# Batches of two key tiles in a sparse attention, and a routing table in buffers of its own

## The chip, the cores and the metric

The kernel runs on one core of a Trainium2 chip. The metric is the device time of one execution in microseconds (us). Before the change the median of three runs is 2298.0 us (2296.09 to 2302.13). The profiled execution, on which all readings of the trace rest, spans 2318.8 us.

The core has five engines that run side by side and meet through semaphores: TensorE (PE, with its weight loads PEld listed apart), VectorE (DVE), ScalarE (ACT), GpSimd (POOL) and SyncE (SP), which here only starts transfers. SBUF is the working memory with 128 partitions; PSUM takes what TensorE writes, in banks of 128 x 512 floats, of which the attention's pools use eight; HBM is the memory outside.

## The reference

One layer: attention of 4096 nodes over the neighbours that an adjacency matrix names, and then a mixture of experts, each with a layer norm ahead and a residual.

```python
# attention; x is (4096, 512), 8 heads of 64, adj is 0/1 and sparse
adj = jnp.maximum(adjacency_matrix, eye)
q, k, v = (jnp.einsum('nd,hdk->hnk', norm(x), W) for W in (Wqs, Wks, Wvs))
scores = jnp.einsum('hqk,hmk->hqm', q, k) * kd ** (-0.5)
scores = scores + IDENTITY_BIAS * eye - MASK_VAL * (1.0 - adj)
att = jax.nn.softmax(scores, axis=-1)
x = x + jnp.einsum('hqm,hmk,hko->qo', att, v, Wo)
# mixture: 8 experts, two for each token, hidden size 512
logits = xf @ Wg + bg                                   # xf = norm(x)
topk_scores, topk_idx = jax.lax.top_k(logits, 2)
topk_w = jax.nn.softmax(topk_scores, axis=-1)
h = gelu(einsum('nd,edh->neh', xf, W1) + b1)            # exact gelu
y = einsum('neh,ehf->nef', h, W2) + b2
x = x + sum over the two chosen experts of topk_w * y
```

All numbers are 32-bit floats.

## The kernel before

It has three stages.

**Stage one** projects q, k and v, stores them in HBM, and makes for each of the 32 tiles of 128 queries a list of the nodes that are a neighbour of any of them. The list is cut into tiles of 128 keys. A tile of keys whose nodes are wanted by the first 64 queries alone, or by the last 64 alone, is a *half* step; the others are *full* steps. How many tiles each query tile has is fixed in the program:

```python
LISTED = [28, 20, 18, 16, 15, 14, 13, 13, ... 8, 8]       # tiles of keys, 363 in all
FIRST_ALONE = [10, 6, 5, 5, 4, ... 2, 2]    # tiles c < this: first half of the queries
SECOND_FROM = [25, 14, 12, 10, 10, ... 5, 5]    # tiles c >= this: second half
```

That gives 229 half steps and 134 full ones. Each query tile also begins with its own 128 nodes (c = -1), a full step: 395 steps.

**Stage two** is the attention. Keys and values are gathered row by row by GpSimd from HBM (`kv`), the adjacency as a mask with them; PE turns the keys (`pk`), ACT copies them to SBUF (`kT`), PE makes the scores (`s`), ACT their exponentials (`e`), DVE masks them and adds them up for the denominators (`acc`), and PE multiplies them with the values into `po`.

```python
AHEAD = 9                                     # kv and mask tiles: 10 buffers
items = [(i, c) for i in range(NT) for c in range(-1, listed[i])]
# PSUM banks: ps_s 3, ps_o 1, ps_k 2 (one tile of two banks), ps_e 2

def turn(n):                                  # keys of one step
    pk = ps_k.tile([P, 2, TB], F32, tag="k", name=f"pk_{n}")
    for p in range(NP):                       # 8 transposes
        for r in range(2):
            half = slice(r * KD, (r + 1) * KD)
            nc.tensor.transpose(
                pk[:, r, ts(p, KD)], kv[n][half, ts(p, P)], ident[half, half])
    nc.scalar.copy(kT[n]..., pk[:, :, : NP * KD]...)

def scores(n):
    if full:                                  # two banks, 64 rows of the array each
        s = [ps_s.tile([P, NP, P], ...) for r in range(2)]
        for p in range(NP):
            for r in range(2):
                rows = slice(r * KD, (r + 1) * KD)
                nc.tensor.matmul(s[r][:, p, :], k[rows, p, :], q_in[i][rows, p, r, :], ...)
        for r in range(2):
            nc.scalar.activation(e...[:, r], s[r], AF.Exp)
    else:                                     # one bank, the whole array, q with zeros
        s = ps_s.tile([P, NP, 2, QH], F32, tag="s", name=f"s_{i}_{c}")
        for p in range(NP):
            nc.tensor.matmul(s[:, p], k[:, p, :], q_in[i][:, p, :, q], ...)
        nc.scalar.activation(e, s.rearrange("p a r q -> p (a r) q"), AF.Exp)

def masked(n):
    nc.vector.tensor_mul(e, e, m.unsqueeze(1).to_broadcast(e.shape))

def values(n):
    if c < 0:
        po[i] = ps_o.tile([P, NP, P], F32, tag="o", name=f"po_{i}")
    for h in range(H):                        # 8 products, 64 columns of the array each
        p, r = divmod(h, 2)
        nc.tensor.matmul(po[i][r * KD : (r + 1) * KD, p, q], v[:, ts(h, KD)], e[:, h, :], ...)
    if c >= 0:
        nc.vector.tensor_add(acc[i][:, :, q], acc[i][:, :, q], e)

for n, (i, c) in enumerate(items):            # the order of the instructions
    begin()
    if n + AHEAD < len(items):
        fetch(n + AHEAD)                      # gathers kv, gathers or loads the mask
    ...
    if c < 0 and i:                           # a new query tile: po of the last one goes out
        osb[i - 1] = single.tile([P, NP, P], F32, tag="o", name=f"o_{i - 1}")
        nc.scalar.copy(osb[i - 1], po.pop(i - 1))
    turn(n + 3); scores(n + 2); values(n)
    later(n)                                  # one piece of the work after a query tile
    masked(n + 2)
```

The pieces after a query tile (`later`) are the sums over `acc`, their reciprocals, `rb`, the product `py` with Wo, the residual, and the routing of the tile's tokens: each token is written to `xs_d` in HBM, once into the region of either expert that it chose (regions of N + 128 rows).

**Between stages two and three** a table says which expert and which 128 rows each of 69 blocks takes. An expert's last block is seldom full, so the rows after its last token are overwritten with blank rows, which point to spare rows of the output. Then a check decides whether the attention has to be done again in a plain way (it isn't with these inputs).

```python
with tc.tile_pool(name="end", bufs=1) as pool, tc.tile_pool(
    name="ps_end", bufs=1, space=PSUM) as psum:
    finish_routing(pool, psum, blank)         # about 20 instructions of DVE, and:
    #   nc.sync.dma_start(out=xs_d[E * R : E * R + P, :], in_=blank)
    #   for e in range(E):
    #       last = nc.values_load(table[:, 2 * NB + e : ...], engines=(SP,), ...)
    #       s = nc.sync.dma_start(out=xs_d[bass.ds(last, P), :], in_=blank)
again = nc.values_load(redo, ...)
with tc.If(again > 0):
    ...
```

**Stage three** takes block by block: load 128 rows (`r`), turn them, multiply by W1, gelu, turn, multiply by W2, weigh, and add to the output with a scatter of GpSimd.

Of the kernel before, what the change touches and what calls it, by code (L numbers as in the profile page):

```python
# [20 lines left out]
P = 128  # L21
# [22 lines left out]
def kernel(  # L44
# [106 lines left out]
    nc.gpsimd.iota(start_e, pattern=[[R, E]], base=0, channel_multiplier=0,  # L151
# [3 lines left out]
    for e in range(1, E):  # L155
# [9 lines left out]
    nth = const.tile([P, NB], F32, name="nth")  # L165
    nc.gpsimd.iota(nth, pattern=[[1, NB]], base=0, channel_multiplier=0,
                   allow_small_or_imprecise_dtypes=True)
# [4 lines left out]
    table = const.tile([1, 2 * NB + E], I32, name="table")  # L172
# [39 lines left out]
    AHEAD = 9  # L212
    items = [(i, c) for i in range(NT) for c in range(-1, listed[i])]
# [21 lines left out]
    def gather_mask(m, i, c):  # L235
        if half_of(i, c) is None:
            gather(m, adjT_rows, mask_of, i, c)
        else:
            gather(m[:, :QH], adjT_halves, mask_of, i, c)
# [4 lines left out]
    def mask_part(m, i, c):  # L244
        return m if half_of(i, c) is None else m[:, :QH]

    def fetch(n):

        i, c = items[n]
        kv[n] = kvp.tile([P, KV], F32, tag="kv", name=f"kv_{i}_{c}")  # L250
        mask[n] = kvp.tile([P, P], F32, tag="mask", name=f"mask_{i}_{c}")
        if c < 0:
            nc.sync.dma_start(out=kv[n], in_=kv_d[ts(i, P), :])
            nc.sync.dma_start(out=mask[n], in_=adjT[i, ts(i, P), :])
            return
        gather(kv[n], kv_d, key_of, i, c)
        if (i, c) in packed:
            nc.sync.dma_start(out=mask_part(mask[n], i, c), in_=packed_at(i, c))
        else:
            gather_mask(mask[n], i, c)  # L260

        if waiting and n % 3 == 0:
            waiting.pop(0)[1]()
# [9 lines left out]
    with tc.tile_pool(name="wqkv", bufs=1) as wp, tc.tile_pool(name="p1", bufs=3) as work, tc.tile_pool(  # L273
# [347 lines left out]
        nc.sync.dma_start(out=out[N : N + P, :], in_=blank[:, :D])  # L621

# [4 lines left out]
        def pack():  # L627
            i, c = ready.pop(0)
            m = work.tile([P, P], F32, tag="mask", bufs=5, name=f"pm_{i}_{c}")
            gather_mask(m, i, c)  # L630
            packed[i, c] = len(packed)
            nc.sync.dma_start(out=packed_at(i, c), in_=mask_part(m, i, c))
# [4 lines left out]
        for u in range(8 * NTB + 1):  # L637
# [38 lines left out]
            if u - 3 in load_at:  # L676
                neighbours(load_at[u - 3])
                if load_at[u - 3] == NT - 1:

                    ap_cm.__exit__(None, None, None)  # L680
                    kv_cm = tc.tile_pool(name="kv", bufs=AHEAD + 1, side="right")
# [9 lines left out]
                    fetch(0)  # L691
            if u == 8 * NTB - 4:
                for n in range(1, AHEAD):
                    fetch(n)
# [115 lines left out]
    def finish_routing(pool, psum, blank):  # L810
# [26 lines left out]
        )  # L837
        expert = pool.tile([P, NB], F32, name="expert")
# [4 lines left out]
        nc.vector.tensor_scalar_mul(first, first, float(P))  # L843
# [5 lines left out]
        nc.vector.tensor_add(many, many, start_e)  # L849
        nc.vector.tensor_copy(table[:, :NB], expert[:1])  # L850
        nc.vector.tensor_copy(table[:, NB : 2 * NB], first[:1])
        nc.vector.tensor_copy(table[:, 2 * NB :], many[:1])
        nc.vector.tensor_add(first, first, number.to_broadcast([P, NB]))

        nc.sync.dma_start(out=xs_d[E * R : E * R + P, :], in_=blank)
        for e in range(E):
            last = nc.values_load(
                table[:, 2 * NB + e : 2 * NB + e + 1], engines=(SP,), min_val=e * R,
                max_val=e * R + N, skip_runtime_bounds_check_because=why,
            )  # L860
            s = nc.sync.dma_start(out=xs_d[bass.ds(last, P), :], in_=blank)
            for t in scatters:
                tc.declare_no_dep(s.ins, t.ins, reason="other rows")
            scatters.append(s)
# [602 lines left out]
```

## Time and profile before

| what | where | us |
|---|---|---|
| median of the runs | times | 2298.0 |
| span of the profiled execution | page | 2318.8 |
| stage one, to the first turned key of stage two | trace, PE | 0 to 449 |
| stage two, to the end of the last value product | trace, PE | 449 to 1715 |
| end of the routing, table, check, first rows | trace, PE | 1715 to 1764 |
| stage three | trace, PE | 1764 to 2311 |

The page gives each engine's busy time over the span, the span in 40 slices, the chain that ended last, and groups of equal instructions with count, busy time, mean duration of one and the engine's idle time just before them. A timeline row of PE joins neighbouring matmuls of one kind: its start, the time from the first start to the last end, and how many. One 32-bit matmul of the program shows as two records. The chain that ended last holds only the final scatter here, so the stages are read from windows and timelines.

### The profile page before, as it was taken

How to read it: one execution, taken by the hardware profiler on the slowest of the kernel's cores; microseconds unless marked ns; L12 is line 12 of the kernel's file. 1: busy time of each engine (PE TensorE's matmuls, PEld its weight loads, DVE VectorE, ACT ScalarE, POOL GpSimd, SP SyncE). 2: the span in 40 equal slices, each digit the busy share in tenths (PEclk: the TensorE clock that was granted, in tenths of full speed). 3: DMA queues.
4: the chain of work that ended last, by engine and by line, in shares of the span. 5: the costliest groups of instructions: out<-in, count | busy, mean ns of one | idle time of the engine just before them, and what ended most of it. 6: DMA issues, size and time to landing. Idle time of an engine off the chain costs nothing. (4 is left out here: it accounts for less than half of the span.)

```text
span 2318.8 us, 48467 instructions
## 1 busy us (share of the span) xinstructions
PE 2104.1 (91%) x18748; PEld 1395.4 (60%) x18748; DVE 1262.0 (54%) x2289; ACT 928.4 (40%) x1703; POOL 1020.0 (44%) x1078
## 2 busy tenths in 40 slices
PE   7988987899999889999999899999975999999997
PEld 3434443487777767777777777777752444444443
DVE  4786666176666656655656666565662323232322
ACT  2544443354545445445445454444531222222221
POOL 1043445666666555555565655556630212211212
PEclk9999999899999899999999999999987999999999
DMA  7778787666777777777787777766766565655554
GB/s 289 314 269 262 258 274 247 204 207 201 228 237 232 209 226 228 219 208 220 220 232 225 239 207 217 234 200 202 203 212 173 134 140 129 135 132 133 136 138 91
DMA packets 213232, 479.04 MB, mean 207 GB/s; under 512 B 49106, under 2 KB 81106, under 8 KB 208900
## 3 DMA queue, kind: packets, MB, share of 16 engines
q0 software_dynamic: 78944, 241.65, 37.2%
q1 hardware_dynamic: 132900, 232.10, 32.6%
q8 instruction: 153, 2.51, 0.4%
q10 hardware_dynamic: 1152, 2.10, 0.3%
q14 instruction: 83, 0.68, 0.1%
HBM read 398.85 MB, written 76.90 MB: 205 GB/s over the span
## 5 line engine op out<-in xcount | busy, mean ns | idle before, releaser
L230 POOL DMA_INDIRECT kv<-kv_d,key_of x363 | 402.8, 1110 | 414.6 <-PE po L993 228.7
L981 DVE TENSOR_TENSOR e<-e,mask 128x512 f32<-128x512 f32 (+1 forms) x363 | 322.2, 888 | 321.8 <-ACT e L973 150.1
L926 ACT COPY kT<-pk 128x512 f32<-128x512 f32 x395 | 232.3, 588 | 375.5 <-PE pk L923 209.7
L993 PE MATMUL po<-e,kv 128*64 128x64 f32 (+1 forms) x5808 | 327.2, 251 | 24.0 <-issue 23.1
L999 DVE TENSOR_TENSOR acc<-acc,e 128x512 f32<-128x512 f32 (+1 forms) x363 | 320.9, 884 | 3.3 <-PE pk L923 2.5
L230 POOL DMA_INDIRECT mask<-in_adjT_dram,mask_of x234 | 280.0, 1197 | 72.9 <-issue 66.7
L1394 POOL DMA_INDIRECT out_dram<-y,r x69 | 107.5, 1557 | 463.8 <-issue 191.3
L993 PEld LDWEIGHTS po<-e,kv 128*64 128x64 f32 x5808 | 254.9, 140 | 76.5 <-issue 33.1
L970 PE MATMUL s<-q,kT 128*128 128x128 f32 x1832 | 283.9, 300 | 2.2 <-issue 1.8
L1358 PE MATMUL ph<-w,xT 128*128 x552 | 251.6, 599 | 0.7 <-ACT xT L209 0.7
L970 PEld LDWEIGHTS s<-q,kT 128*128 128x128 f32 x1832 | 237.4, 202 | 20.0 <-issue 3.5
L1387 PE MATMUL py<-w,hT 128*128 x552 | 248.4, 593 | 0.9 <-DVE hT L1372 0.9
L923 PE MATMUL pk<-ident,kv 64*128 64x64 f32 x2904 | 177.8, 240 | 43.4 <-issue 21.5
L923 PEld LDWEIGHTS pk<-ident,kv 64*128 64x128 f32 x2904 | 124.6, 142 | 114.4 <-issue 77.1
L230 POOL DMA_INDIRECT pm<-in_adjT_dram,mask_of x129 | 125.0, 969 | 155.2 <-DMA packed_h<-pm 73.9
L361 DVE TENSOR_REDUCE flags<-adjT 128x64 f32<-128x4096 f32 x32 | 141.1, 4411 | 67.4 <-DMA adjT<-in_adjT_dram 67.3
L963 ACT ACTIVATE e<-s 128x512 f32<-128x512 f32 x268 | 146.9, 597 | 72.9 <-PE po L993 28.6
L973 ACT ACTIVATE e<-s 128x512 f32<-128x512 f32 x229 | 137.9, 602 | 90.7 <-PE s L970 55.8
L958 PE MATMUL s<-q,kT 64*128 64x128 f32 x2144 | 164.0, 284 | 3.8 <-issue 2.3
L1392 DVE TENSOR_TENSOR y<-py,bb 128x512 f32<-128x512 f32 x69 | 47.7, 692 | 219.2 <-PE py L1387 209.7
L1358 PEld LDWEIGHTS ph<-w,xT 128*128 128x128 f32 x552 | 100.5, 192 | 101.3 <-issue 100.2
L1387 PEld LDWEIGHTS py<-w,hT 128*128 128x128 f32 x552 | 99.6, 190 | 101.1 <-issue 99.9
(600 smaller groups left out, 2604.3 us busy)
## 6 DMA issues: line engine op xcount, KB each, us to landing
adjT<-in_adjT_dram SPq DMA_DIRECT2D x32, 2048.0 KB
bb<-in_L_ffn_b_dram SPq DMA_DIRECT2D x138, 256.0 KB
r<-xs_d SPq DMA_DIRECT2D x69, 258.0 KB
kv_d<-kv SPq DMA_DIRECT2D x32, 512.0 KB
xt<-in_x_dram SPq DMA_DIRECT2D x32, 256.0 KB
qT_d<-qT SPq DMA_DIRECT2D x8, 1024.0 KB
q<-qT_d SPq DMA_DIRECT2D x64, 128.0 KB
xr<-in_x_dram SPq DMA_DIRECT2D x32, 256.0 KB
```

What stands on the lines that cost most here:

```text
L230: nc.gpsimd.indirect_dma_start(out=to, out_offset=None, in_=src, in_offset=bass.IndirectOffsetOnAxis(ap=of[:, at[i] + c : at[i] + c + 1], ...
L361: nc.vector.tensor_reduce(flags[g][:, :, j, :], adj_in.pop(i).rearrange("p c (h q) -> p h c q", h=2), axis=AX.X, op=ALU.max,)
L923: nc.tensor.transpose(pk[:, r, ts(p, KD)], kv[n][half, ts(p, P)], ident[half, half])
L926: nc.scalar.copy(kT[n].rearrange("k p (r j) -> k r p j", r=2), pk[:, :, : NP * KD].rearrange("k r (p j) -> k r p j", p=NP),)
L958: nc.tensor.matmul(s[r][:, p, :], k[rows, p, :], q_in[i][rows, p, r, :], start=True, stop=True,)
L963: nc.scalar.activation(e.rearrange("p (a r) q -> p r a q", r=2)[:, r], s[r], AF.Exp)
L970: nc.tensor.matmul(s[:, p], k[:, p, :], q_in[i][:, p, :, q], start=True, stop=True)
L981: nc.vector.tensor_mul(e, e, m.unsqueeze(1).to_broadcast(e.shape))
L993: nc.tensor.matmul(po[i][r * KD : (r + 1) * KD, p, q], v[:, ts(h, KD)], e[:, h, :], start=(c < 0 and p == 0), stop=(c == listed[i] - 1), s ...
L999: nc.vector.tensor_add(acc[i][:, :, q], acc[i][:, :, q], e)
L1358: nc.tensor.matmul(ph, xTs[b][:, c, :], w1[:, bass.ds(es[b], 1), c, :], start=(c == 0), stop=(c == DC - 1),)
L1387: nc.tensor.matmul(py, hTs[b][:, c, :], w2[:, bass.ds(es[b], 1), c, :], start=(c == 0), stop=(c == HC - 1),)
```

## The change

It does two things.

**Attention by batches.** Two half tiles of keys of the same query tile, as a rule one for each half of the queries, become one unit with one mask tile and one tile of exponentials; two full tiles (the own tile counts as one) become one batch of two units. There are 207 batches: 102 of two half tiles, 78 of two full ones, 8 of a full and a half, 17 of one half and 2 of one full. A batch's keys are turned into one PSUM tile and copied at once; the scores of the next batch are made ahead of the values of this one. The number of products is the same. The half steps' scores go over the whole array as before, two banks for a pair.

**The table.** It is made after the check, in buffers of its own. A block that would reach past its expert's last token begins earlier, so that it ends with it; rows that another block has already are sent to spare rows of the output. So no blank rows are written after the tokens; nine blank stores at the start of the kernel fill the 128 rows ahead of each expert's region and after the last.

```diff
-    AHEAD = 9
-    items = [(i, c) for i in range(NT) for c in range(-1, listed[i])]
+    KEPT = 10
+    units, batches = [], []
+    for i in range(NT):
+        parts = {h: [c for c in range(listed[i]) if half_of(i, c) is h] for h in (0, None, 1)}
+        pairs = [[a, b] for a, b in zip(parts[0], parts[1])]
         ... (leftover halves two by two; full ones and the own tile two by two, in between)
-    def fetch(n):
+    def fetch(until):
+        while len(fetched) < min(until, len(keys_of)):
             ... (mask of a pair: one tile, 64 columns each; kv as before)
+                mask[n] = kvp.tile([P, P], F32, tag="mask", bufs=9, name=f"mask_{i}_{c}")
@@ start of the kernel
+        for e in range(E + 1):
+            nc.sync.dma_start(out=xs_d[e * R : e * R + P, :], in_=blank)
@@ attention
-        def turn(n):
-            kT[n] = work.tile([P, NP, P], F32, tag="kT", bufs=3, name=f"kT_{n}")
+        def turn(batch):
+            k = work.tile([P, 2, NP, P], F32, tag="kT", bufs=2, name=f"kT_{batch[0]}")
             ... (8 transposes for each tile of keys, one copy for the batch)
         def masked(n):
-            m = mask_part(m, i, c)
-            nc.vector.tensor_mul(e, e, m.unsqueeze(1).to_broadcast(e.shape))
+            m = mask.pop(n)[:, :w].unsqueeze(1).to_broadcast([P, H, w])
+            nc.vector.tensor_mul(es[n], es[n], m)
+        def summed(n):
+            if at_q == [j * m for j in range(len(cs))] and m * len(cs) == P:
+                nc.vector.tensor_add(acc[i], acc[i], es[n])
+                return
+            for j, c in enumerate(cs):
+                a = acc[i][:, :, queries(i, c)]
+                nc.vector.tensor_add(a, a, es[n][:, :, ts(j, m)])
         def values(n):
             ... (8 products for each tile of keys)
+            if last:
+                osb[i] = single.tile([P, NP, P], F32, tag="o", name=f"o_{i}")
+                nc.scalar.copy(osb[i], po.pop(i))
-            turn(n + 3); scores(n + 2); values(n); later(n); masked(n + 2)
+            begin(b)
+            fetch(k0 + KEPT)                  # k0: first key tile of batch b
+            for n in batch[: 0 if own else None]:
+                summed(n)
+            coming = batches[b + 2 : b + 3]
+            for n in nxt:                     # the units of batch b + 1
+                if half_of(units[n][0], units[n][1][0]) is not None and coming:
+                    turn(coming.pop())
+                scores(n)
+                exps(n)
+                if coming:
+                    turn(coming.pop())
+                masked(n)
+            for n in batch:
+                if own:
+                    summed(n)
+                values(n)
+            later(b)
@@ between the stages
-    with tc.tile_pool(name="end", bufs=1) as pool, tc.tile_pool(...) as psum:
-        finish_routing(pool, psum, blank)
     again = nc.values_load(redo, ...)
     with tc.If(again > 0):
         ...
+    with tc.tile_pool(name="ps_end", bufs=1, space=PSUM) as psum:
+        finish_routing(endp, psum)
@@ finish_routing
-        nc.sync.dma_start(out=xs_d[E * R : E * R + P, :], in_=blank)
-        for e in range(E):
-            last = nc.values_load(...)
-            s = nc.sync.dma_start(out=xs_d[bass.ds(last, P), :], in_=blank)
+        ends = pool.tile([P, NB, E], F32, name="ends")
+        nc.vector.tensor_mul(ends, past, more_e.unsqueeze(1).to_broadcast([P, NB, E]))
+        nc.vector.tensor_reduce(till, ends, axis=AX.X, op=ALU.add)
+        nc.vector.tensor_tensor(begin, first, till, op=ALU.min)
+        nc.vector.tensor_tensor(mine, begin, first, op=ALU.is_ge)
         ... (some ten small instructions more)
@@ stage three, each block
+                nc.vector.scalar_tensor_tensor(to[:, 0:1], ..., spare, mine[:, b : b + 1],
+                    op0=ALU.subtract, op1=ALU.mult)
+                nc.vector.tensor_add(to[:, 1:2].bitcast(I32), to[:, 0:1], spare)
```

The pieces after a query tile also go through fewer steps (four batches instead of six steps) and no longer keep the routing jobs waiting in the steps in which they themselves use PE.

## The prediction

> **What bounds the kernel now.** I read the page for the stages, then busy time by windows, then the groups by shape inside the attention (600 to 1700 us), then PE's timeline, and last the gap at 1715 to 1764 us. Two windows, in the attention and around the gap (start:end, length, busy us of PE, PEld, DVE, ACT, POOL, then the granted clock, DMA share, GB/s):
>
> ```profile
> 1000.00:1200.00 200.00, 184.56 (x2346) 147.77 (x2343) 118.56 (x186) 91.18 (x182) 113.67 (x103) 0.94 0.77 221
> 1900.00:2100.00 200.00, 200.00 (x622) 98.70 (x622) 60.49 (x128) 47.04 (x78) 40.02 (x26) 1.00 0.59 134
> ```
>
> The mixture (second line) is PE without a hole at full clock; the change adds nothing to PE there. In the attention PE is busy for 92%, DVE for 59%, and nothing else more but the transfers (77%). So PE sets the time, but busy time hides what it does. The groups of PE and DVE in the attention by shape, and ACT's copy on the page (busy us, mean ns of one | idle before):
>
> ```profile
> L970 PE MATMUL s<-q,kT 128*128 128x128 f32 x1608 | 247.9, 299 | 2.2 <-issue 1.8
> L923 PE MATMUL pk<-ident,kv 64*128 64x64 f32 x2496 | 153.0, 240 | 31.3 <-issue 19.4 <-ACT kT L926 7.8 <-ACT less L787 3.3
> L981 DVE TENSOR_TENSOR e<-e,mask 128x512 f32<-128x512 f32 x201 | 139.0, 692 | 189.4 <-ACT e L973 130.7 <-issue 51.1 <-ACT kT L926 7.2
> L958 PE MATMUL s<-q,kT 64*128 64x128 f32 x1770 | 135.1, 284 | 3.2 <-issue 2.3 <-ACT e L963 0.6
> L981 DVE TENSOR_TENSOR e<-e,mask 128x1024 f32<-128x1024 f32 x110 | 134.6, 1224 | 96.5 <-ACT e L963 87.6 <-issue 8.2
> L993 PE MATMUL po<-e,kv 128*64 128x128 f32 x1728 | 119.4, 280 | 0.1
> ```
> ```profile
> L926 ACT COPY kT<-pk 128x512 f32<-128x512 f32 x395 | 232.3, 588 | 375.5 <-PE pk L923 209.7
> ```
>
> PE's timeline late in the attention, at full clock (start, us from first start to last end):
>
> ```profile
> 1696.13 0.46 PE L923 MATMUL pk<-ident,kv 64*128 64x64 f32 x8
> 1696.43 1.11 PE L958 MATMUL s<-q,kT 64*128 64x128 f32 x16
> 1697.47 0.69 PE L993 MATMUL po<-e,kv 128*64 128x64 f32 x16
> 1698.08 1.16 PE L1031 MATMUL rb<-rinv,spread 128*128 128x128 f32 x8
> ...
> 1701.89 0.46 PE L923 MATMUL pk<-ident,kv 64*128 64x64 f32 x8
> 1702.29 1.16 PE L970 MATMUL s<-q,kT 128*128 128x128 f32 x8
> 1703.37 1.09 PE L993 MATMUL po<-e,kv 128*64 128x128 f32 x16
> 1704.40 3.70 PE L1040 MATMUL py<-wo,o 128*128 128x512 f32 x8
> ```
>
> Differences of starts say what a group costs: transposes 0.40 us ahead of a half step's scores (1701.89 to 1702.29) and 0.30 ahead of a full one's; half scores 1.08, full scores 1.04; value products 0.61 for 64 queries, 1.03 for 128. A half step is 0.40 + 1.08 + 0.61 = 2.09 us, a full one 0.30 + 1.04 + 1.03 = 2.37. With 229 half and 166 full steps (134 and 32 own tiles): 479 + 393 = 872 us. After each query tile come sums, rb, py, two routing products and a transpose, about 6.5 us by the same reading, 208 in all. The sum is 1080 of the 1266 us from 449 to 1715. The rest is waits and slow clock: PE's waits between 480 and 1760 us add up to some 97 us, led by
>
> ```profile
> PE po L993 <- issue: 25.4, 55, 1.1
> PE pk L923 <- issue: 20.4, 43, 1.6
> PE po L993 <- ACT o L1156: 17.4, 15, 3.6
> PE pk L923 <- ACT kT L926: 10.5, 16, 1.7
> ```
>
> and a mean granted clock of 0.963 over the attention's windows costs 0.037 x 1220 = 45 us.
>
> **A fixed part in each group.** A row's length less the mean of one record is the distance from its first to its last start. Transposes: (0.46 - 0.24)/7 = 0.031 us for each, 0.25 for eight, so of 0.40 (before half scores) 0.15 is something else, of 0.30 (before full scores) 0.05. Half scores: (1.16 - 0.30)/7 = 0.123, 0.98 for eight, leaves 0.10 of 1.08. Full scores: (1.11 - 0.28)/15 = 0.055, leaves 0.16. Values of 128 queries: (1.09 - 0.28)/15 = 0.054, leaves 0.16 of 1.03. Values of 64 queries: with 0.234 as the mean, (0.69 - 0.23)/15 = 0.030, leaves 0.13. So some 0.38 us of a half step and 0.37 of a full one are paid for passing from one kind of group to the next, whatever their length. Between transposes (64 rows, 128 columns of the array) and full scores (the same shape) it nearly vanishes.
>
> [...] 0.10 to 0.16 us where the shape changes, 0.05 where it doesn't. [...] the rows above have 692 and 1224, so joining two saves 0.16 us. [...] the waits called "issue" above, in the middle of groups whose operands are all there, look like PE short of instructions. The change doesn't shorten PE's program.
>
> **The change, part by part.**
>
> *Fewer passages on PE.* A batch of two halves does 16 transposes, 16 records of scores and 32 of values, and pays the fixed part once: 102 x 0.38 = 39 us. A batch of two full tiles goes scores, transposes, scores, values, values; the first two passages are between equal shapes, so about 0.05 + 0.16 + 0.16 stand for twice 0.37: 78 x 0.36 = 28 us. Together -67 us, all on PE's path. The other 27 batches gain nothing I count.
>
> *The own tile's wait.* po's copy is now issued right after the last values, and two to three us of transposes and scores come ahead of the next po. Of 17.4 us for o and 10.5 for kT I take 20 off.
>
> *A new wait for banks.* Two full tiles need four score banks of three. The fourth waits for an exponential (0.6 us, some 0.25 more to start); the 16 transposes between cover about 0.5. I take 0.35 us in each of 78 batches: +27 us.
>
> *DVE and ACT*, beside PE: masks 229 x 0.692 against 102 x 1.224 + 25 x 0.692, -17 us; sums -14 us; ACT's copies, with 0.588 us for 512 elements and 0.268 for 128 (so about 1.0 for 1024), some -33 us. Not counted.
>
> *The gap.* Now:
>
> ```profile
> 1746.98 0.17 DVE L815 COPY many<-pn 128x8 f32<-128x8 f32 x1 [7.96 <-DMA out_dram<-xr]
> ```
> ```profile
> 1747.44 0.36 SPq L855 DMA_DIRECT2D xs_d<-blank  x1
> 1749.58 6.49 SPq L861 DMA_DIRECT2D xs_d<-blank  x8
> 1761.17 0.37 SPq L1344 DMA_DIRECT2D r<-xs_d  x1
> ```
>
> DVE waits for a buffer that a store still reads, makes the table in 5.9 us (to 1752.9), SP writes blanks until 1756.1, and 5.1 us later, check included, the first rows are asked for; they land in 3 us. After: the check's input is there at 1737.6; check and loads 5.1 us; the table, with two more passes over 568 elements at 0.75 and eight small ones, 5.9 + 3.1 = 9.0: rows asked for at 1751.7, -10 us. W2's transfers, at 370 GB/s and more, end at 1745, so they don't stand in the way.
>
> *Elsewhere.* Nine stores of 258 KB at the start are 2.3 MB, 8 us of transfers at 290 GB/s, in a stage that waits little for DMA: +2 us. Two small DVE instructions a block in the mixture, DVE busy 30%: 0.
>
> Sum: -67 - 20 + 27 - 10 + 2 = -68; 2298 - 68 = 2230 us.
>
> **The rivals.**
>
> *Gathers come too late.* kv has ten buffers as before, but a batch holds two, and the next is turned two batches after its gather may start, about 11 us, where it was six steps, 19 us. For: GpSimd needs 1.10 us for a kv gather and 1.20 for a mask, with 0.3 between, some 4.5 us a batch, in order. Against: counting each gather's packets in order in the trace, a kv gather has landed 4.4 us after its start (median; 6.7 the longest), so the second of a batch is there after 7 to 8 us. If it misses by 0.5 us in every batch: +100, about 2330.
>
> *The three banks and ACT's order.* Between the exponentials of two full tiles ACT now copies 1024 elements, 1.0 us; if the chain scores, exponentials, copy, exponentials, mask becomes the pace, each such batch loses 1 us instead of 0.35: 2280.
>
> *Instructions are the supply.* If PE, rid of passages, only reaches the next refill sooner, half of the 67 us returns as "issue": 2263.
>
> *Better than the sum.* Fewer holes may keep the clock up: all 45 us of slow clock and the small waits gone would make it 2170.
>
> **Range and chances.** The passages are measured and sit on the bound engine; what may return is 20 to 50 us through the banks and the supply, what may come on top about as much. 2165 to 2280 for 8 in 10. The line of 2% is 2252, 22 us over my figure: faster 0.68, same 0.28, slower 0.04, the last for late gathers.
>
> **What would show it.** Right: rows of 16 transposes and 32 value records in PE's timeline, each followed by one gap; the same count of PE records; attention of about 1205 us; the wait for o gone; first rows of the mixture some 10 us sooner after the check's input. The bank wait shows as PE s waiting for ACT e at L958's successor. Wrong: pk waiting for DMA kv; "issue" well above 46 us; a clock under 0.95; stage one longer by more than 5 us.

## The result, and the profile after

The changed kernel takes 2334.64 us (median; 2332.36 to 2342.02) beside 2297.05 us for the kernel before: ratio 1.0166, interval 1.0138 to 1.0195. It was predicted to be 68 us shorter and is 38 us longer.

The profile of the kernel before printed above spans 2318.8 us, some 20 more than the median of its times; that of the changed kernel spans 2330.6. A second pair of profiles, made later side by side (e17 and e18 below), agrees with the medians of its own runs. The table holds both; every boundary is the start of a PE group: first transpose of keys, last value product, the product that makes the check's input, first product with W1.

| us | before | after | before (e17) | after (e18) |
|---|---|---|---|---|
| stage one | 449.0 | 450.7 | 448.7 | 447.5 |
| attention | 1265.7 | 1271.3 | 1108.9 | 1145.3 |
| tail: last values to the check's input | 22.7 | 40.0 | 19.7 | 40.5 |
| gap: check's input to the first product with W1 | 28.6 | 20.3 | 31.5 | 19.8 |
| mixture to the end | 552.8 | 548.2 | 547.5 | 548.0 |
| span | 2318.8 | 2330.6 | 2156.3 | 2201.1 |

The kernel before took about 2300 us in some sessions and about 2160 in others. I call them sessions of 2300 and of 2160, and compare within a session, or by the ratio to the kernel before in the same session. The prediction was made in one of 2300.

The changed kernel's window in the attention, as it was shown of before (start:end, length, busy us of PE, PEld, DVE, ACT, POOL, granted clock, DMA share, GB/s):

```profile
1000.00:1200.00 200.00, 178.06 (x2426) 148.10 (x2424) 122.61 (x169) 90.10 (x160) 113.81 (x104) 0.96 0.73 225
```

In the attention PE's busy time has gone from 184.6 to 178.1 of 200 us while it got through more records (2426 for 2346): shorter groups, longer waits.

PE's groups of scores and transposes in the attention by shape (busy us, mean ns of one | idle before), and PE's waits between 480 and 1760 us (us in total, times, longest):

```profile
L1009 PE MATMUL s<-q,kT 128*128 128x128 f32 x1592 | 212.0, 286 | 0.3 <-issue 0.3
L997 PE MATMUL s<-q,kT 64*128 64x128 f32 x2241 | 210.7, 301 | 61.0 <-ACT e L1017 23.2 <-issue 17.4 <-ACT acc L1017 10.8
...
L957 PE MATMUL pk<-ident,kv 64*128 64x64 f32 x2488 | 121.5, 229 | 15.8 <-issue 8.1 <-DMA kv<-kv_d,key_of 7.4 <-ACT kT L962 0.2
```
```profile
PE po L1050 <- issue: 39.4, 84, 1.1
PE s L997 <- ACT e L1017: 26.3, 23, 2.9
PE s L997 <- issue: 20.0, 23, 2.3
...
PE pk L957 <- issue: 9.8, 22, 1.0
```

The waits of before for po's copy and for kT (27.9 us) are gone but for 2.0. The waits for keys from memory add up to 7.4 us. In their place the scores of full tiles, which had waited 3.2 us, wait 61 us, 34 of it for exponentials that free a bank; and the waits called "issue" in these lines have grown from 46 to 69 us. Counted over all of PE's groups, and without the attention's first 13 us, they grew from 56 to 73. The start is left out because one wait there changes its name and not its cause:

```profile
460.53 1.12 PE L957 MATMUL pk<-ident,kv 64*128 64x64 f32 x16 [9.08 <-issue]
```

These transposes start as ACT's copy of the keys before them ends (459.46 to 460.47), and the profile of before puts the same wait, 7.5 us at its start, down to kT. PE's timeline shows the new wait in its least form:

```profile
1695.64 1.16 PE L997 MATMUL s<-q,kT 64*128 64x128 f32 x16
1696.64 0.66 PE L957 MATMUL pk<-ident,kv 64*128 64x64 f32 x16
1697.13 0.44 PE L997 MATMUL s<-q,kT 64*128 64x128 f32 x2
1698.00 1.16 PE L997 MATMUL s<-q,kT 64*128 64x128 f32 x14 [0.43 <-ACT e L1017]
```

Two full tiles: the first's 16 score records, 16 transposes, then two records of the second tile run and the other 14 stand until an exponential has emptied a bank.

And the gap:

```profile
1759.39 0.31 DVE L812 CAST slot_i<-slot 128x2 int32<-128x2 f32 x1 [13.90 <-DMA xs_d<-rows,slot_i]
...
1769.23 0.17 DVE L844 COPY many<-pn 128x8 f32<-128x8 f32 x1 [3.98 <-PE pn L842]
...
1777.52 0.37 SPq L1419 DMA_DIRECT2D r<-xs_d  x1
```

From the count (1769.2) to the first rows asked for (1777.5) it takes 8.3 us, where the table with the blanks took 14.2 before. But everything there starts later: the last routing waited 13.9 us for a scatter of rows.

### The profile page after: what moved, and what is told of

The parts are those of the page before. It is cut to its first block, busy times and chain, and to the rows that moved or that the text cites. A ratio compares the mean times of both kernels' runs of the same rounds, so it can differ in the third digit from the quotient of the medians.

```text
span 2330.6 us, 47457 instructions
## 1 busy us (share of the span) xinstructions
PE 2070.2 (89%) x18748; PEld 1401.1 (60%) x18748; DVE 1278.8 (55%) x2239; ACT 895.5 (38%) x1515; POOL 1006.2 (43%) x1079
## 3 DMA queue, kind: packets, MB, share of 16 engines
q8 instruction: 153, 2.51, 0.4%
## 5 line engine op out<-in xcount | busy, mean ns | idle before, releaser
L1022 DVE TENSOR_TENSOR e<-e,mask 128x1024 f32<-128x1024 f32 (+1 forms) x261 | 306.0, 1174 | 321.7 <-ACT e L1017 257.4
L1050 PE MATMUL po<-e,kv 128*64 128x64 f32 (+1 forms) x5808 | 307.9, 253 | 41.4 <-issue 37.2
L997 PE MATMUL s<-q,kT 64*128 64x128 f32 x2656 | 248.2, 300 | 67.6 <-ACT e L1017 26.7
L1476 POOL DMA_INDIRECT out_dram<-y,to x69 | 107.8, 1562 | 449.1 <-ACT y L1468 445.0
L962 ACT COPY kT<-pk 128x1024 f32<-128x1024 f32 (+1 forms) x207 | 201.9, 975 | 248.0 <-PE pk L957 86.1
L1032 DVE TENSOR_TENSOR acc<-acc,e 128x1024 f32<-128x1024 f32 x227 | 274.9, 1211 | 2.9
L997 PEld LDWEIGHTS s<-q,kT 64*128 64x128 f32 x2656 | 203.0, 199 | 101.2 <-issue 37.9
L1009 PE MATMUL s<-q,kT 128*128 128x128 f32 x1832 | 244.4, 287 | 0.3 <-issue 0.3
L957 PE MATMUL pk<-ident,kv 64*128 64x64 f32 x2904 | 141.7, 229 | 26.8 <-issue 17.9
L1468 ACT ACTIVATE y<-y,gate 128x512 f32<-128x512 f32 x69 | 49.8, 722 | 217.0 <-DVE y L1467 217.0
## 6 DMA issues: line engine op xcount, KB each, us to landing
q<-qT_d SPq DMA_DIRECT2D x64, 128.0 KB
```

The lines of the kernel that those rows point to most:

```text
L957: nc.tensor.transpose(pk[:, r, ts(t * NP + p, KD)], kv[n, j][half, ts(p, P)], ident[half, half],)
L962: nc.scalar.copy(k.rearrange("k j p (r c) -> k r (j p) c", r=2)[:, :, :m], pk.rearrange("k r (m c) -> k r m c", c=KD)[:, :, :m],)
L1009: nc.tensor.matmul(s[:, p], k[:, p, :], q_in[i][:, p, :, queries(i, c)], start=True, stop=True,)
L1022: nc.vector.tensor_mul(es[n], es[n], m)
L1032: nc.vector.tensor_add(acc[i], acc[i], es[n])
L1050: nc.tensor.matmul(po[i][r * KD : (r + 1) * KD, p, queries(i, c)], v[:, ts(h, KD)], e[:, h, ts(j, m)], start=(c < 0 and p == 0), stop=(las ...
```

## Where the attention's time lies

For the pair of one session I took each group of PE (consecutive records of one line) from its start to the next group's start, and for each kind of group (line, count, following line) its lower quartile at full clock as its length without a wait. Value products for 64 and for 128 queries are separate kinds. Summed over all groups of the attention, up to the group that follows the last value products (us; after, that group starts 2 us after their end, so the sum is 2 us above the attention of the first table):

| | before (e17) | after (e18) |
|---|---|---|
| transposes of keys | 148.0 | 128.0 |
| scores of halves | 250.1 | 229.3 |
| value products | 311.0 | 286.8 |
| scores of full tiles | 173.5 | 203.3 |
| products after a query tile, routing | 203.1 | 195.7 |
| waits beyond these, at full clock | 12.0 | 39.0 |
| excess in groups at half clock, waits there included | 11.2 | 65.3 |
| sum | 1109.0 | 1147.4 |

The first three lines are the passages: -65.0 us. The fourth is the bank in its least form: a second full tile's scores take 1.44 us (the lower quartile), not 1.04, and with 77 such batches that is some +30. So the sum of the groups does fall, by 43 us. What eats it stands in the last two lines: +81 us of waits and half clock.

## The experiments

**Session of 2160: four parts by themselves.** e1 puts the values of the batch before between the scores of two full tiles:

```
             for k, n in enumerate(nxt):
                 ... scores(n); exps(n); turn; masked(n)
+                if k == 0 and len(nxt) == 2:
+                    for m in todo: values(m)      # todo = batch; own tiles are summed first
+                    todo = []
```

> Changed kernel, with the values of batch b put between the scores of the two full tiles of batch b + 1, so that the second scores start some 1.5 us after the first instead of 0.5. Theory A (three score banks for four: PE waits at the second scores for the first exponential and whatever ACT has ahead of it; 2.1 us on average for a group that needs 1.04): the 68 us of idle time ahead of the full scores nearly vanish and some slow clock with them, time 80 to 110 us under the changed kernel, 2225 to 2255. Rival B (PE is held by its supply of instructions, whose count is the same): the idle time moves to 'issue', within 20 us of the changed kernel, 2315 to 2335. Rival C (the slow clock comes from elsewhere): half of the gain, about 2285.

Measured: 2189.16 us, ratio 1.0123 (1.0101 to 1.0144). That is some 17 us under the changed kernel beside it (e4), where 80 to 110 were expected of the bank alone.

e2 leaves full tiles in batches of one:

```
-        wide = [wide[j : j + 2] for j in range(0, len(wide), 2)]
+        wide = [[u] for u in wide]
```

> Changed kernel, with full tiles of keys as batches of one; only half tiles go in pairs. Two banks are needed at a time, so theory A's wait is gone, and so is the saving in passages of 78 x 0.36 = 28 us; the look-ahead between full steps shrinks to one tile of keys. Theory A with enough look-ahead: 2334 - 90 + 28, about 2272. If the look-ahead is too short (scores, exponentials 1.2, mask 1.2 us against transposes, scores and values of one tile, 2.4 us), PE waits for DVE's mask in the values and the time is 2330 or more.

Measured: 2171.33 us, ratio 1.0047 (1.0032 to 1.0062).

e3 is the kernel before with the table's part of the change alone (rows from P on, blanks at the start, the table behind the check).

> Kernel before, with only the second part of the change: table after the check in its own buffers, no blank rows after the tokens, nine blank stores at the start, two small instructions of DVE in each block. My step says -10 us in the gap and +2 at the start: 2289. Rival: the check and the table now follow one another, and the start loses more: 2297 or above.

Measured: 2152.8 us, ratio 0.9948 (0.993 to 0.9967).

e4 was meant to take the scatters of the tail out of their chain, each waiting until the one before has landed (in the changed kernel's first profile GpSimd stands 2.14 to 6.79 us ahead of each of the last seven of the eight):

```
-                        waiting.pop(0)[1](True)
+                        waiting.pop(0)[1](chain())   # chained only at the order's end
```

> Changed kernel, with the routing scatters of the last groups issued without waiting for one another once the attention's order has ended (they write different rows). Theory D (the tail is long because eight scatters run one after the other while the eight loads of W2 fill the queues, and a buffer that they hold stops DVE for 14 us): the routing ends 12 to 17 us earlier, 2318 to 2323. Rival (the tail is bound by the chain of the last query tile on PE, DVE and ACT): within 3 us of 2334.

Measured: 2206.47 us, ratio 1.0207 (1.0183 to 1.0231). The edit missed its mark: the eight scatters that matter are issued inside the attention's fixed order, where they stayed chained, and the tail is 41 us as in the changed kernel. It tells nothing of the tail and serves as one more run of the changed kernel.

What follows: the table's part gains 8 us (14 in e12 below); all that is lost is lost in the attention and its tail. With the values between, the waits for banks fall and the attention is 15 us shorter (1126.1 for 1141.0 in e4), but PE still waits for keys, which rival 1 of the prediction had named (us in total, times, longest; first e1, then e2):

```profile
PE pk L957 <- DMA kv<-kv_d,key_of: 35.8, 20, 10.0
```
```profile
PE pk L957 <- ACT kT L962: 37.2, 46, 9.3
```

With full tiles alone the keys come in time (7.0 us of waits), but a batch of one tile is only one step ahead of its copy (before the change scores ran two steps ahead and transposes three), so kT is waited for, 37 us by the transposes and 13 by scores.

**Session of 2300: three suspects, and the changed kernel itself.** e5 is the changed kernel.

> The changed kernel itself, unaltered, beside the kernel before: the measure for the next three runs. If its loss belongs to the program, the ratio is again 1.014 to 1.021 though the chip's pace is another (the run with the whole attention unchanged gave 1.0207 beside a kernel before of 2161 us). If the loss came from the supply of instructions (waits called issue: 46 us before, 79 us after in the first profiles), the ratio falls to 0.99 or less wherever these waits are missing.

Measured: 2336.09 us, ratio 1.0131 (1.0076 to 1.0185). The loss belongs to the program; it is there with the issue waits (69 us of them in the attention after its start) and without.

e6 gathers both tiles of keys of a batch ahead of the masks:

```
-            else:
-                gather_mask(m, i, c)
+            else:
+                later_masks.append((m, i, c))      # gathered two at a time, after the keys
```

> The changed kernel with the two gathers of keys of a batch issued ahead of the two gathers of masks. The second gather of keys starts some 1.2 us sooner. If late gathers cost (rival 1; PE waited 36 to 38 us for kv in two runs, mostly 0.5 to 2.7 us at a time, of which 10 to 11 us in one wait behind chained scatters), about 15 to 20 us go: ratio to the changed kernel 0.991 to 0.993. If gathers are hidden and the waits would come back elsewhere, within 4 us of the changed kernel.

Measured: 2336.42 us, ratio 1.0139 (1.0092 to 1.0186): nothing. Beside it, e5 has no wait for keys in its list of PE's waits, so the run had nothing to gain. It doesn't test the gathers; e9 does, together with two other mends.

e7 moves ACT's copy of the next keys behind the second tile's exponentials:

```
-            nc.scalar.copy(k..., pk...)                  # in turn()
+            copies.append(lambda: nc.scalar.copy(k..., pk...))
 ...
+                if n == nxt[-1] and copies:               # after exps(n)
+                    copies.pop()()
```

> The changed kernel with ACT's copy of the next batch's keys after the exponentials of the second full tile, not between the two tiles' exponentials. If ACT's order delays the bank (rival 2: the second tile's scores take 2.1 us in the mean where 1.04 are needed), the second exponentials start about 1 us sooner, and the group falls to about 1.5 us: 0.3 to 0.5 us x 80 = 25 to 40 us less on a chip where it waits, at least 10 us less here. If the bank is bound by the first exponential alone, nothing: within 4 us. It may also cost: the next batch's scores wait for the later copy.

Measured: 2399.41 us, ratio 1.0403 (1.0359 to 1.0447): 63 us worse than e5. From the second tile's first score to the first value product took 2.01 us in e5 (mean of the 63 batches at full clock) and takes 1.83 (54 batches): the copy between the exponentials holds the bank for a small part only. But the next scores now wait for it, and the next transposes for another 25 us (the first line of e7's waits of PE):

```profile
PE s L999 <- ACT kT L964: 38.4, 37, 4.5
```

Rival 2 falls in the form in which it was put, and another part of ACT's order takes its place (below).

e8 puts a memset between the chained scatters:

```
-                        waiting.pop(0)[1](True)
+                        nc.gpsimd.memset(between, 0.0)
+                        waiting.pop(0)[1]()
```

> The changed kernel with a small memset on GpSimd between the scatters of rows that it issues inside the attention's order, so that one need not wait until the one before has landed. If the chained scatters make the tail (40 us from the last value product to the check's input against 21 to 23), and the one long wait for keys of 10 to 11 us, then the tail falls to about 25 us and that wait goes: 20 to 26 us less, ratio to the changed kernel 0.988 to 0.991. If the tail is set by the late routing alone, 0 to 5 us less.

Measured: 2328.77 us, ratio 1.0114 (1.0076 to 1.0153). That is 7 us under e5, where 20 to 26 were expected, and the intervals of the two overlap; what is plain is the tail in the profiles, which falls from 40.1 to 28.5 us. GpSimd's timeline, the second and the eighth scatter of e5 and then the eighth of e8:

```profile
1721.51 0.99 POOL L828 DMA_INDIRECT xs_d<-rows,slot_i  x1 [3.28 <-DMA xs_d<-rows,slot_i]
...
1755.50 0.97 POOL L828 DMA_INDIRECT xs_d<-rows,slot_i  x1 [2.46 <-DMA xs_d<-rows,slot_i]
```
```profile
1732.43 0.97 POOL L828 DMA_INDIRECT xs_d<-rows,slot_i  x1 [0.19 <-issue]
```

The eight start within 38.3 us in e5 (from 1717.2) and within 11.0 in e8 (from 1721.5). The chain was in the kernel before as well; there the last group of four tiles was routed early enough for its scatters to run beside the attention. A routing job now runs once a batch, of which there are 207, where there were 395 steps, so this group is routed later and the chain lies bare, among W2's loads (asked for from 1723.8 to 1738.9 us in the changed kernel's first profile). e2 supports this: it has the chain as it was but more batches, the last of its chained scatters starts at 1578.3 and most of them beside the attention, which ends at 1574.6, and its tail is 25 us.

**Session of 2160: the mends together.** e9 has e1's values between, e6's order and e8's memset. e10 also turns the next keys ahead of the first full tile's scores, as before the change:

```
-                if half_of(units[n][0], units[n][1][0]) is not None and coming:
-                    turn(coming.pop())
-                scores(n); exps(n)
-                if coming:
-                    turn(coming.pop())
+                if coming:
+                    turn(coming.pop())
+                scores(n); exps(n)
```

e11 has e2's full tiles alone, this turn ahead, e6's order and e8's memset: of the change to the attention only the pairs of halves remain. e12 is e3 again.

> The changed kernel with three mends: the values of the batch before between the scores of two full tiles (no wait for a bank), both gathers of keys ahead of the masks, a memset between the chained scatters. If the bank wait, the late gathers and the chained tail are what ate the passages' 67 us, their mends add up: tail 28 us for 40 (-12), bank wait on a chip as slow as the last one -60 or so of full-clock time in 76 batches (second tile's scores to the values 1.6 us more than needed with slow clock), on the faster one -15; gathers -2 to -15. Ratio to the kernel before 0.975 to 0.99. If holes of PE only move to another place (instructions as the supply), the ratio stays above 1.0.

> As the run before, and the next batch's keys are turned ahead of the scores of the first full tile, as before the change, so that ACT's copy comes ahead of the exponentials. If the copy between the exponentials delays them or the next batch, 5 to 15 us less than the run before; if the keys are then wanted some 1.3 us too early for their gathers, 10 to 30 us more. It gives up the two passages between equal shapes (0.1 us each in 78 batches, 8 us).

> Full tiles in batches of one and turned ahead of their scores as before the change, pairs of halves as in the change, with the mends for gathers and scatters. Only the 102 pairs of halves should gain: 39 us of passages, with no bank wait and the tail near 25 us. With the table's 8: ratio 0.98 to 0.985. If pairs of halves too bring nothing (their gathers, copies and masks twice as long bring their own waits), 0.995 as the table alone.

> The kernel before with the table's part of the change alone, beside the others of this call. -8 us of gap and +2 of stage one, whatever the chip's pace: ratio 0.995 to 0.998.

Measured: e9 2161.74 us, ratio 0.9975 (0.9962 to 0.9988); e10 2169.39, 1.0004 (0.9991 to 1.0017); e11 2137.33, 0.9856 (0.984 to 0.9873); e12 2153.16, 0.9929 (0.9912 to 0.9945).

The mends take back what the change lost (1.0207 in e4, 0.9975 here), though not the 0.975 to 0.99 expected, and e9 with all its shorter groups is still behind the table alone (0.9929). Its longest entry in PE's waits says why, and the same entry of e11 what is different there:

```profile
PE pk L963 <- DMA kv<-kv_d,key_of: 28.1, 18, 4.7
```
```profile
PE pk L963 <- DMA kv<-kv_d,key_of: 2.3, 2, 1.1
```

Ten buffers of keys that are taken and given back two at a time give the gathers too little lead (28 us); with full tiles alone they suffice (2.3 us; in e2, which differs from e4 in this alone, 7.0 for 38.5). More buffers were not tried. Asking for keys first was worth at most 8 us, and e10, which wants them earlier still, waits 31 us. e11 keeps the gain of the halves (scores 250.1 to 229.3, values 311.0 to 296.0, transposes 148.0 to 124.3 us), its half clock is back near that of before, and beside them it beats both kernels.

**Session of 2300: the same again, and the other half.** e13 batches full tiles by two and half steps by one, without the mends:

```
-        pairs = [[a, b] for a, b in zip(parts[0], parts[1])]
+        pairs = [[c] for c in parts[0] + parts[1]]
```

(the lines that join what is left over are gone, and the first fetch asks for nine tiles of keys). e14 is e1, e15 is e9 and e16 is e11 again.

> The other half of the change alone: full tiles in batches of two as in the change, half steps in batches of one, with the table's part and none of the mends. Passages of 78 batches should give 28 us by the sum, the table 8; the bank wait costs what it costs. If the batches of two full tiles are where the change loses (bank, gathers, holes at half clock), this is no better than the changed kernel: ratio to the kernel before 1.01 to 1.03. If both kinds of pairs lose alike, about 1.005.

> The changed kernel with the values of the batch before between the scores of two full tiles, once more beside other runs. On a chip whose kernel before takes some 2300 us, where the second tile's scores wait 1.1 us in the mean, the bank is worth 40 to 60 us if rival 2 is right: ratio 0.985 to 0.995 where the changed kernel had 1.0131. On one whose kernel before takes some 2160 us again 1.012.

> All three mends, beside the run before: gathers and chain. On a chip of 2160 us again 0.9975; on one of 2300 us, where keys came late only twice, 10 to 15 us below the values between alone, by the tail.

> Pairs of halves alone with the mends, once more. On a chip of 2160 us again 0.9856. On one of 2300 us: the passages' 39 us and the table's 8 if the supply of instructions doesn't take the gain back, 0.98; if PE only reaches the next wait for instructions sooner (rival 3), half of it, 0.988 to 0.992.

Measured: e13 2405.95 us, ratio 1.0476 (1.043 to 1.0523); e14 2312.83, 1.0062 (1.0046 to 1.0078); e15 2293.23, 0.9956 (0.9941 to 0.9972); e16 2325.82, 1.0116 (1.0073 to 1.0158).

e13 is worse than any theory had it, and not clean: a half step alone is now one step ahead of its copy and its exponentials, and PE waits 29 us for kT and 24 for exponentials. It doesn't weigh the pairs of full tiles by themselves. e14 and e15 show the bank, and then the chain and the late keys together, as parts of the loss here too (1.0131 in e5, then 1.0062, then 0.9956). e14's bank brings less than the ratio of 0.985 to 0.995 expected; between e14 and e15 the tail falls by 9 us, and e14's two waits for keys, 10.9 us, are gone. e16 is the surprise: the best of the session of 2160 loses here. The head of its waits of PE:

```profile
PE pk L963 <- issue: 26.8, 40, 11.0
PE po L1056 <- issue: 23.7, 71, 0.9
```

Its groups without waits sum to as little as in the other session (1031 and 1027 us), but waits called issue are back in its attention, where e11 had none: 68 us of them without the one of 11.0, which is again the copy at the attention's start. The kernel before had 56 in its profile of another session of 2300. Against that profile e16's groups wait 43 us more at full clock, 12 of them issue, and half clock costs 24 us more. The issue waits that rival 3 expected are therefore a part of what took e16's gain, and the rest stays open.

**Session of 2160: a clean pair.** e17 is the kernel before, e18 the changed one.

> The kernel before, unaltered, for a second profile of it: the first one's span, 2318.8 us, lies 20 us above the median of its times. Ratio 1. On a chip of 2300 us the attention should be some 1245 to 1265 us with waits called issue of about 50 us; on one of 2160 us some 1113 us, as with the table alone, with none.

> The changed kernel beside it on the same chip. On a chip of 2300 us again 1.013 to 1.017 and, by the two profiles, attention longer by 10 to 25 us, tail by 17; on one of 2160 us 1.02, attention longer by 30, tail by 20. In both the groups' sum without waits is some 40 us smaller (66 of passages less 28 of the bank), and the waits and half clock some 60 to 80 us larger.

Measured: e17 2160.21 us, ratio 1.0002 (0.9994 to 1.001); e18 2203.17, ratio 1.021 (1.0193 to 1.0227). From PE's waits in the attention of e17 (the longest entry) and of e18:

```profile
PE pk L923 <- ACT kT L926: 16.7, 8, 7.7
```
```profile
PE pk L957 <- DMA kv<-kv_d,key_of: 38.3, 22, 11.4
PE s L997 <- ACT e L1017: 12.8, 19, 3.4
...
PE po L1050 <- DVE e L1022: 9.9, 2, 6.4
```

These holes cost a second time. PE in e18, and below it the window's granted clock (the column before the DMA share):

```profile
1354.30 0.69 PE L957 MATMUL pk<-ident,kv 64*128 64x64 f32 x8 [2.34 <-DMA kv<-kv_d,key_of]
1354.92 3.30 PE L1009 MATMUL s<-q,kT 128*128 128x128 f32 x16
```
```profile
1354.16:1357.57 3.41, 3.27 (x20) 3.16 (x21) 0.25 (x1) 1.56 (x2) 2.57 (x3) 0.50 1.03 331
```

There is a hole of 2.34 us, then 3.41 us at half clock, in which 16 score records take 3.30 us instead of 2.05. In e17's attention there are three such periods, 27 us in all; in e18's thirteen, 85 us. All but the first, at the attention's start, begin within a hole of PE or within 1 us after one; nine of these holes are only 1.55 to 3.41 us long, the others 4.24 to 11.44. What they have in common in this pair is a share and not a length. The periods are whole multiples of 3.41 us and begin on one grid of that step, as they do in the attentions of the first pair (3.41, 6.83, 10.24 us and longer); in the step of the grid ahead of each of the twelve PE stood idle for 57% of the time or more, and in every other step at full clock for 44% or less (in e17 60% or more and 46% or less). A hole of 2.66 us that the grid cuts into two parts, 40 and 38% of their steps, passed without a fall. In other profiles the two ranges overlap (e11: falls from 45% on, and none after a step with 50%; before: from 35% on, and none after one with 45%), so this is no sharp line.

One more wait showed in this pair. The copy called test, which reads a query tile's sums, now stands at the start of a batch, ahead of the exponentials, and waits there for DVE's reciprocal, which has its own queue of masks ahead. PE and then ACT in e18:

```profile
776.91 1.74 PE L997 MATMUL s<-q,kT 64*128 64x128 f32 x14 [3.41 <-ACT e L1017]
```
```profile
776.00 0.28 ACT L1102 ACTIVATE test<-sums 128x128 bf16<-128x128 f32 x1 [6.20 <-DVE rinv L1100]
```

ACT idled 6.2 us, during the last 3 of which full banks waited for it; PE stood 3.4 us, and the clock fell for the next 3.4. Over the attention ACT waits 76.7 us in 29 places for this reciprocal, in e17 never. Such a wait need not cost PE anything: e11, the fastest kernel of its session, has 55 us of them. What moving that copy alone would bring was not tried.

## Why the prediction was wrong

The step that failed is the treatment of what is not busy time. The sum took the shorter groups as gained on PE's path, took 20 us off the waits and left the clock as it was. By the reckoning of the second table, the groups themselves came out as summed: -39 us in the first pair and -43 in the clean one, for -67 + 27 = -40. But the waits at full clock grew by 2 and by 27 us where -20 was predicted, the excess at half clock grew by 42 and by 54 where nothing was, and the tail, which had no term, by 17 and by 21. These make up the whole miss, 80 us between the first two profiles and 113 in the clean pair. Term by term:

- **Fewer passages (-67).** Right: -65 us in the clean pair, some -59 in the first one by the same reckoning. The fixed part per group held: by the prediction's own reckoning, e18 (from 600.47 us on) pays 0.13 us for a group of 16 transposes, 0.10 for 16 records of half scores and 0.13 to 0.15 for 32 of values. What it consists of was not shown.
- **The own tile's wait (-20).** Right where it was predicted: 27.9 us of waits for o and kT became 2.0 in the first pair, from 480 us on; in the clean one, without the attention's first 13 us, 14.0 became 2.4. The copy at the start itself grew dearer: PE waits 10.7 us for it where it waited 7.7.
- **The wait for banks (+27).** Right as the least case (+30: 0.40 us in 77 batches for 0.35 in 78), mis-sized as a whole. It assumed that ACT is free when the bank is full. In the changed kernel's first profile ACT is not, in a good part of the batches: from the first tile's last score to the first exponential it takes 0.3 us when ACT is free, 0.8 in the mean (batches at full clock). Waits of 45 us for e, acc and test stand in PE's list there, 21 of them, for e and acc, in e18. ACT's order has a part in it, as rival 2 said, but the copy of keys only a small one (e7). The copy of sums that waits for DVE stands ahead of such a wait in the timeline above; how much of the 45 us it makes was not measured.
- **Gathers.** The sum had 0 for them: "a kv gather has landed 4.4 us after its start", 11 us of lead. It failed in that it added up one gather's way and not what delays its start: a buffer given back in pairs, masks and scatters ahead in GpSimd's order, among them chained ones (one wait of 11.4 us; in e9, with the memset, the longest is 4.7). In e18 38 us, in e9 still 28; in the prediction's own session 7. Rival 1 was right in kind, and too large with 100.
- **The supply of instructions (rival 3, +33).** In the first pair issue waits grew from 56 to 73 us after the attention's start: 18 of the rival's 33 us. In sessions of 2160 there are next to none, before or after; so the rival can hold in one kind of session only, and e18's loss shows that the change loses without it. That these waits are a lack of instructions was a guess and was not shown: "issue" says only that the profile shows nothing that the engine waited for, and the DMA queue called instruction has the same 153 packets (2.51 MB) with these waits (before, e5) and with 0.5 us of them (e4).
- **The clock.** The sum left the slow clock as it was, and rival 4 had hoped for less of it. It grew: from 63 to 105 us of excess in half-clock groups in the first pair, from 11 to 65 in the clean one, waits inside these groups included. This is the largest term missing. In the clean pair it follows the holes, so it counts them a second time; that it is no cause of its own is argued from this order in time.
- **The tail.** No term at all: +17 and +21 us. The prediction did not ask when the last routing jobs run. e8 shows 12 us of it to be the chain of scatters; the rest goes with later routing, since e2, which has more batches, has a tail of 25 us.
- **The gap (-10), the start (+2), the mixture (0).** Right: -8 and -12, +2 and -1, -5 and 0.

Put by who is waited for, the 113 us of the clean pair (68 less predicted, 45 more measured) are late keys 38, exponentials and masks about 31, the tail 21, and half speed for 58 us longer some 29: 119, by waits that partly overlap. The mends show that the bank, the order of the gathers and the chain together are worth the loss (1.0207 to 0.9975, 1.0131 to 0.9956); how it divides among them rests on the lists of waits.

## What to carry to other kernels

When a bound engine's work is batched to save fixed parts, look first at what the batch doubles elsewhere: buffers given back in pairs, exponentials owed at once, side jobs that come half as often. A few tenths of a microsecond per wait are not all that it costs; in e18 a hole of 2.34 us was followed by 3.41 at half clock, so here a saving in PE's busy time was kept only where no new hole opened (e11). Batch the part whose lead is large enough (here the halves) and leave the other alone, and measure it where it will run: the same version was 1.4% faster in one session and 1.2% slower in another.

## What the runs showed that I had not expected

- The same program, the kernel before, took 2302 us in one session and 2160 in another, on the same chip (e5 to e8 and e17 to e18). Nearly all of the difference lies in the attention (1265.7 us and 1108.9), as issue waits of PE (56 us and none) and half clock (106 us and 27). DVE shows it too, ahead of its masks: 63.5 us of issue in one profile and 5.0 in the other. Stage one and the mixture are equal within 6 us. What makes a session one or the other stays open.
- Half clock began at or shortly after holes of only 1.55 to 3.41 us in nine places of e18, though not after each hole as short: of 21 holes over 1 us in e18's attention 13 lie in a half-clock period or up to 3.5 us ahead of one. In this pair the share of idle time in a step of 3.41 us, 57% and more against 44% and less, sorts these places, and the length of a hole does not.
- Two exponentials with the copy of keys behind them (e7) cost 63 us more than with the copy between, though they freed the banks sooner (second scores to values in 1.83 us for 2.01).
